# Four-layer graph network: early steps of layer 1 ahead of its norm, checks of layer 2 in other places, and a hyperbolic preparation with X0's numbers on GpSimd

## The chip, the cores and the metric

The kernel runs on one core of a Trainium2 chip. Five engines work side by side, each with a queue of its own that it takes in order: PE (TensorE, matrix products and transposes), ACT (ScalarE, activations with function tables that are loaded in sets), DVE (VectorE), POOL (GpSimd) and SP (SyncE, which issues most transfers). The metric is the device time of one execution in microseconds, the median of several runs. The profile describes one other execution.

## The reference, cut to what matters

Four layers share one adjacency matrix of 3327 by 3327 zeros and ones (0.5% ones) and a feature matrix x of 3327 by 64. Each layer normalizes x, clips it at zero, computes something over the graph and adds it to x.

```
h = relu(layernorm(x)); x = x + hyperbolic(h, adj, att_W, att_b)      # layer 0
h = relu(layernorm(x)); x = x + decay(h, adj, weight, bias)           # layer 1
h = relu(layernorm(x)); x = x + gat_and_gru(h, adj, adj, ...)         # layer 2
h = relu(layernorm(x)); x = x + hyperbolic(h, adj, r, w_att, b_att)   # layer 3

# hyperbolic: attention over pairs, times the hyperbolic logarithm of each pair
adj_att = sigmoid(left + right.T) * adj
support = einsum('ij,ijd->id', adj_att, logmap(x[:, None, :], x[None, :, :]))
return proj(expmap(x, support))

# decay: neighbours weighted by 0.5 to the power of how many neighbours come after them (at most 100)
w = mask * where(pos > 0, 0.5 ** (k - pos), 0);  return w @ (h @ weight) + bias

# gat_and_gru: sums over neighbours without the diagonal; two GRU cells
node_support = [(A > 0) @ h, (A < 0) @ h]
edge_output = gru_cell(node_support, h, ...)
node_output = gru_cell(softmax over neighbours @ (h @ W), h, ...)
return d_edge * edge_output + d_node * node_output
```

## The kernel before, in words

The 3327 nodes are padded to 3328 = 26 tiles of 128 (T = 26, P = 128, D = 64). The kernel takes a fast path that holds for an adjacency of zeros and ones and for small numbers; flags that this path collects (`zo`, `ok`) decide at the end whether its result stands, and a general path follows in the program otherwise.

**Layers 0 and 3** are `hyperbolic_series`. A preparation normalizes, makes two half-precision parts of the features (`hi`, `lo` in `Xp`), transposes them tile by tile on PE into `XT` (7 groups of four tiles, each copied out of PSUM by ACT or DVE in turn), computes the time-like coordinate X0 of every point and its half-precision parts on DVE (`of_x0`, `of_e`, `of_f`, L454 to L470), transposes these into `XE`, makes `left` and `right`, spreads `left` over all partitions with PE (`of_left`, L514 to L522), and computes seven small numbers per node that are needed at the end of the layer (L538 to L544). `keep_busy` issues products whose result nobody reads. After it runs a loop over 104 pieces (4 column chunks, 26 row tiles): sigmoid on ACT (L575), times the mask on POOL (L577), products on PE (L588, L589), a square on ACT (L595), two operations on DVE (L600, L601), sums on PE (L610, L618). A short tail of small operations ends the layer; in layer 3 it calls Tanh and then loads the table of Sqrt (L739 to L742).

**Layer 1** is `plain_decay`. It runs over 52 steps, 2 column halves by 26 row tiles from the last to the first. In each step DVE makes a mask from a loaded piece of the adjacency (L1326) and tests the same piece for zeros (`zeros`, L1248). PE counts neighbours with a triangular matrix (L1333, `after` and `rest`), ACT takes 2 to the power of minus the count (L1339, an Exp), PE sums (L1350). For 13 of the 52 steps (`LATE` = 0, 1, 7, 11, ... 47) the test for zeros is left out here. Ahead of the steps stands the norm (`norm_relu`, L131 to L143), which goes from DVE to ACT (Square, L135; Sqrt, L98) and back. The pieces are loaded seven ahead.

**Layer 2** is `plain_gat`. It has its own norm, then on PE 26 products with the masks (L1518, in order of falling b), in between small jobs from a table `todo`: transposes (`turn`), degrees (`degrees`) and their inverse (`inverse`, on ACT with Relu, Ln and Exp and the table of Sigmoid afterwards). The 13 tests that layer 1 left out are done here, one at every even b, from pieces loaded again into three buffers. Behind them come the GRU steps u = 0 to 7, which begin with `take` (L1538, L1539): it moves the sums out of PSUM, on ACT and on DVE.

The order of instructions on ACT, DVE, PE and (in the first two) POOL is that of the source inside a block `tc.manual_schedule`; outside of such blocks, and between them, a scheduler places what is ready. An ACT instruction that needs another function set gets a table load in front, which the building of the program puts there. `table_of` (L117 to L119) issues a one-element activation only to have a table loaded early:

```
def table_of(f, after=None):
    A.activation(spare, one_c if after is None else after, f)
```

Of the kernel before, what the change touches and what calls it, by code (L numbers as in the profile page):

```python
# [46 lines left out]
def tile_gnn4(ctx: ExitStack, tc: tile.TileContext, x, adjT, att0, b0, w1, bias1, w_gat, a_gat,  # L47
# [274 lines left out]
    def hyperbolic_series(r, params, ok, masks=None, done=None):  # L322
# [18 lines left out]
        with ExitStack() as st:  # L341
# [53 lines left out]
            with tc.tile_pool(name="hsp", bufs=1) as tp, tc.tile_pool(name="hsps", bufs=2, space=PSUM) as ps, \  # L395
                    tc.manual_schedule(engines={mybir.EngineType.Activation, mybir.EngineType.DVE,
                                                mybir.EngineType.PE, mybir.EngineType.Pool}):
                Xe = tp.tile([P, T, KE + 9], F16, name="Xe")
# [11 lines left out]
                H, R, sq, sr = [tp.tile([P, T, D], F32, name=n) for n in ("H", "R", "sq", "sr")]  # L410
# [43 lines left out]
                def of_x0():  # L454
                    V.scalar_tensor_tensor(x0, x2, 1.0, ia, op0=OP.add, op1=OP.mult)
                    V.tensor_scalar(x0s, x0, SX, None, op0=OP.mult)
                    V.tensor_copy(p0[:, :, 0], x0s)
                    V.tensor_sub(rest, x0s, p0[:, :, 0])
                    V.tensor_copy(p0[:, :, 1], rest)
                    V.tensor_sub(rest, rest, p0[:, :, 1])  # L460
                    V.tensor_copy(p0[:, :, 2], rest)

                def of_e():
                    for k, src in ((0, h0.to_broadcast([P, T, 3])), (3, m0.to_broadcast([P, T, 2])), (5, l0)):
                        V.tensor_copy(E[:, :, k:k + src.shape[-1]], src)

                def of_f():
                    for k, src in ((0, p0), (3, hm0), (5, h0)):
                        V.tensor_scalar(Fe[:, :, k:k + src.shape[-1]], src, -1.0, None, op0=OP.mult)
                    G.tensor_copy(F, Fe)  # L470
# [7 lines left out]
                def to_columns16(dst, src, rows, odd, between=()):  # L478
                    between = list(between)
                    for t0 in range(0, T, 4):  # L480
                        n = min(4, T - t0)
                        pt = ps.tile([P, 4 * P], F16, name="pt", bufs=4)
                        for k in range(n):
                            PE.transpose(pt[:rows, k * P:(k + 1) * P], src[:, t0 + k, :], ident_h)  # L484
                        if t0 // 4 % 2 == odd:
                            V.tensor_copy(dst[:, t0 * P:(t0 + n) * P], pt[:rows, :n * P])
                        else:
                            A.activation(dst[:, t0 * P:(t0 + n) * P], pt[:rows, :n * P], AF.Copy)
                        if between:
                            between.pop(0)()  # L490

                junk, pe = [ps.tile([P, W], F32, name=n, bufs=1) for n in ("junk", "pe")]

                def keep_busy(n):

                    for _ in range(n):
                        PE.matmul(junk, ident_h, hi[:, :8, :], start=True, stop=True)

                keep_busy(4)
                to_columns16(XT, Xp[:, :, :2 * D], P, 1,  # L500
                             (of_x0, of_e, of_f, lambda: V.tensor_copy(Xe[:, :, :D], hi), of_z))
                columns(chunks[0])

# [8 lines left out]
                c = chunks[0]  # L512

                def of_left():  # L514

                    for o, to in ((0, junk), (1, pe)):
                        for i in range(c[1]):
                            t = o * HT + c[0] + i
                            PE.matmul(to[:, i * P:(i + 1) * P], left[:, t:t + 1].to_broadcast([P, P]), ident,
                                      start=True, stop=True)  # L520
                    V.tensor_copy(leftB[c][:, 0, :], junk[:, :c[1] * P])
                    A.activation(leftB[c][:, 1, :], pe[:, :c[1] * P], AF.Copy)  # L522

                to_columns16(XE, Xe, KE + 9, 0, (lambda: None, of_left))
                for o in range(2):
                    pt = ps.tile([P, 4 * P], F16, name="pt", bufs=4)
                    for i in range(c[1]):
                        PE.transpose(pt[:KE, i * P:(i + 1) * P], Xp[:, o * HT + c[0] + i, D:], ident_h)
                    V.tensor_copy(XF[c][:, o, :], pt[:KE, :c[1] * P])
                PE.transpose(pe[:T, :P], left, ident)  # L530
                keep_busy(6)
                A.activation(LT, pe[:T, :P], AF.Copy)
                nc.sync.dma_start(left_row, LT)
                V.tensor_copy(X0[:, :, 0], x0)
                V.scalar_tensor_tensor(good, x2, X2_MIN, nodes, op0=OP.is_ge, op1=OP.mult)
                V.reduce_sum(ok, good, axis=AX.X)
# [7 lines left out]
                V.tensor_scalar(small["bh"], ax, 0.5, isqc, op0=OP.mult, op1=OP.mult)  # L544

# [143 lines left out]
            with tc.tile_pool(name="hse", bufs=1) as tp:  # L689
# [28 lines left out]
                if r is None:  # L718


                    f = MIN_NORM
                    by, g = new("by"), new("g")
                    V.tensor_scalar(by, v2, -f * f, 1.0, op0=OP.mult, op1=OP.add)
                    V.tensor_scalar(g, by, MIN_NORM, None, op0=OP.max)
                    V.reciprocal(g, g)
                    V.tensor_mul(t, root, g)
                    A.activation(th, t, AF.Tanh)
                    V.tensor_mul(th, th, rr)
                    V.tensor_mul(y2, th, th)
                    stt(vh, vh, 2.0 * f, th, op0=OP.mult, op1=OP.mult)  # L730
                    V.tensor_mul(y2, y2, x2)
                    stt(d, v2, f * f, y2, op0=OP.mult, op1=OP.mult)
                else:

                    V.tensor_scalar(t, v2, 1e-8, None, op0=OP.max)
                    ti = inverse_root(tp, t, "ti")
                    V.tensor_mul(t, t, ti)
                    V.tensor_scalar(t, t, um, None, op0=OP.max)
                    A.activation(th, t, AF.Tanh)  # L739
                    table_of(AF.Sqrt, th[:, :1])  # L740
                    V.reciprocal(ti, t)
                    V.tensor_mul(th, th, ti)  # L742
                    V.tensor_mul(y2, th, th)
                    stt(vh, vh, 2.0, th, op0=OP.mult, op1=OP.mult)
                    V.tensor_mul(y2, y2, v2)
                    V.tensor_mul(d, y2, x2)
# [526 lines left out]
    def plain_decay(masks, zo, deg, wt, bias, gru, ball_of_r):  # L1273
# [11 lines left out]
        with ExitStack() as st:  # L1285
# [24 lines left out]
            with tc.tile_pool(name="pdacc", bufs=1, space=PSUM) as pa, tc.manual_schedule(  # L1310
# [54 lines left out]

                K_ = len(steps)
                make_mask(0)
                make_mask(1)
# [15 lines left out]
                for o in range(2):  # L1384
                    cnt[o] = pa.tile([P, 2, 512], F32, name=f"cnt{o}")
                for k in range(K_ + 2):
                    c, b = steps[min(max(k, 0), K_ - 1)]
                    if 0 <= k < K_:
                        counts(k, 0, after)
                        weights(k, 0)  # L1390
                    if 0 <= k - 1 < K_:
                        counts(k - 1, 1, rest)
                        if steps[k - 1][1] == 0:
                            degrees(steps[k - 1][0], 1)
                    if 0 <= k < K_:
                        counts(k, 1, after)
                        weights(k, 1)
# [4 lines left out]
                    if 0 <= k < K_:  # L1402
# [7 lines left out]
                    if k == 1:  # L1410
                        late()
# [19 lines left out]
    def plain_gat(masks, zo, deg, first, wg, gru):  # L1431
# [8 lines left out]
        with ExitStack() as st:  # L1440
# [10 lines left out]
            wk = st.enter_context(tc.tile_pool(name="pgl", bufs=3))  # L1451
# [4 lines left out]
            with tc.tile_pool(name="pgp", bufs=1) as tp, tc.tile_pool(name="pgacc", bufs=1, space=PSUM) as pa, \  # L1456
# [4 lines left out]

                hn = tp.tile([P, T, D], F32, name="hn")
# [25 lines left out]
                def degrees(k):  # L1488

                    cs = slice(k * BK, (k + 1) * BK)  # L1490
# [4 lines left out]
                    V.tensor_sub(deg[:, cs], deg[:, cs], dg)  # L1495

                def inverse():
# [8 lines left out]
                    table_of(AF.Sigmoid, r0[:, :1])  # L1506
                    V.scalar_tensor_tensor(deg, deg, -1.0, r0, op0=OP.mult, op1=OP.mult)
                    V.scalar_tensor_tensor(deg, deg, 2.0, r0, op0=OP.add, op1=OP.mult)

                todo = {T - 4: lambda: turn(0), T - 6: lambda: degrees(0), T - 8: lambda: turn(4),  # L1510
                        T - 9: lambda: degrees(1), T - 11: lambda: turn(8), T - 12: lambda: degrees(2),
                        T - 14: lambda: turn(12), T - 15: lambda: degrees(3), T - 17: inverse}
                for b in range(T - 1, -1, -1):
# [9 lines left out]
                    if b % 2 == 0:  # L1523
                        same = wk.tile([P, 2, CW], BF, name="same", bufs=1)
                        k = LATE[(T - 1 - b) // 2]
                        zeros(same, late.pop(0), zo[:, k:k + 1])


# [173 lines left out]
```

## Time and profile before

| | |
|---|---|
| median of 3 runs | 819.15 us (821.02, 819.15, 817.87) |
| profiled execution, its own time | 818.34 us |
| span of its instructions | 816.6 us |
| mean granted TensorE clock | 0.924 of full speed |
| busy: PE, DVE, ACT, POOL | 81%, 87%, 71%, 51% |
| layer 0: preparation, loop, tail | 0 to 35, 35 to 264, 264 to 284 us |
| layer 1 | 284 to 425 us |
| layer 2 | 428 to 527 us |
| layer 3: preparation, loop, tail | 529 to 560, 560 to 789, 790 to 811 us |

All times inside the span are microseconds from its start. In a row of a timeline the first number is the start, the second the busy time (of all that are merged in the row), then engine, line, operation, output <- input, shapes and how often; in brackets the idle time of the engine before it and what released it. Rows of neighbouring like instructions are merged, so a row can reach past the start of the next.

### The profile page before, as it was taken

The numbers are of one execution on the slowest core, as the hardware profiler recorded it, in microseconds if no ns is written. First come the engines' busy times: TensorE is split into PE (matmuls) and PEld (weight loads), VectorE is DVE, ScalarE is ACT, GpSimd is POOL, SyncE is SP. The second block draws the span as 40 slices with busy tenths as digits, with TensorE's granted clock in tenths as the row PEclk, the third lists the DMA queues.
The fourth block names the chain that finished last, engine by engine and source line by source line (L and its number), as shares of the span: only waits on it lengthen the run. The fifth ranks groups of instructions, "written<-read, shape, count | busy, mean of one in ns | idle before, by whom it ended". The sixth has DMA issues, their size and how long they took to land. (4 is left out here: it accounts for less than half of the span.)

```text
span 816.6 us, 11802 instructions
## 1 busy us (share of the span) xinstructions
PE 659.8 (81%) x4215; PEld 252.1 (31%) x4215; DVE 709.1 (87%) x985; ACT 576.2 (71%) x729; POOL 416.1 (51%) x296
## 2 busy tenths in 40 slices
PE   0799999999999049989993995427999999999960
PEld 0522233333332024435441651214222333333320
DVE  6789999989998899998967567996899999999976
ACT  2678888878886367777782575255888888888862
POOL 2299988989987050003120000004687777787730
PEclk9989999999999569999996997757999999999995
DMA  3567676776664739998913541001001001000001
GB/s 75 164 203 219 205 212 184 205 213 196 196 189 120 292 131 327 372 379 298 367 36 132 187 151 50 1 4 45 1 1 34 1 1 36 1 1 2 1 2 46
DMA packets 57621, 107.84 MB, mean 132 GB/s; under 512 B 8752, under 2 KB 33488, under 8 KB 57552
## 3 DMA queue, kind: packets, MB, share of 16 engines
q1 hardware_dynamic: 53200, 106.97, 40.5%
q10 hardware_dynamic: 4352, 0.02, 0.3%
q8 instruction: 35, 0.57, 0.3%
q14 instruction: 34, 0.28, 0.1%
HBM read 103.72 MB, written 0.88 MB: 128 GB/s over the span
## 5 line engine op out<-in xcount | busy, mean ns | idle before, releaser
L595 ACT ACTIVATE y<-slot,shift_c 128x768 f32<-128x768 f32 (+1 forms) x208 | 197.4, 949 | 68.4 <-ACT sig L575 48.6
L601 DVE TENSOR_TENSOR sig<-slot,sig 128x768 f32<-128x768 f32 (+1 forms) x208 | 213.2, 1025 | 23.3 <-POOL sig L577 2.1
L600 DVE SCALAR_TENSOR_TENSOR slot<-y,slot 128x768 f32<-128x768 f32 (+1 forms) x208 | 212.1, 1020 | 9.1 <-ACT y L595 9.0
L577 POOL TENSOR_TENSOR sig<-adj,sig 128x768 f32<-128x768 f32 (+1 forms) x104 | 201.9, 1962 | 28.1 <-ACT sig L575 26.0
L575 ACT ACTIVATE sig<-leftB,right 128x768 f32<-128x768 f32 (+1 forms) x208 | 204.1, 981 | 3.5 <-DVE bh L544 3.5
L577 POOL TENSOR_TENSOR sig<-mask,sig 128x768 f32<-128x768 fp8e4 (+1 forms) x104 | 174.6, 1680 | 61.6 <-ACT sig L575 57.6
L610 PE MATMUL slot<-sig,Xr 128*64 128x384 f32 (+1 forms) x832 | 188.3, 541 | 16.8 <-DVE sig L601 16.8
L588 PE MATMUL slot<-XC,XT 128*128 128x384 f16 (+1 forms) x416 | 142.9, 344 | 5.2 <-DVE sig L601 3.5
L589 PE MATMUL slot<-XF,XE 73*128 73x384 f16 (+1 forms) x416 | 142.0, 341 | 0.0
L1339 ACT ACTIVATE w<-cnt,ebias 128x832 bf16<-128x832 f32 x104 | 93.7, 950 | 30.7 <-PE cnt L1333 30.7
L1248 DVE TENSOR_SCALAR_CACHE_REDUCE same<-adj 128x1664 bf16<-128x1664 f32 x52 | 97.5, 1876 | 3.6 <-DMA adj<-in 3.4
L618 PE MATMUL slot<-sig,X 128*32 128x384 f32 (+1 forms) x832 | 96.0, 533 | 0.0
L610 PEld LDWEIGHTS slot<-sig,Xr 128*64 128x64 f32 x832 | 43.1, 135 | 122.5 <-DVE sig L601 83.4
L1333 PE MATMUL cnt<-mask,after 128*128 128x416 fp8e4 x208 | 54.8, 347 | 22.7 <-DVE mask L1326 19.8
L588 PEld LDWEIGHTS <-XT 128*128 128x128 f16 x416 | 40.8, 98 | 96.1 <-issue 70.7
L191 POOL TENSOR_TENSOR mask<-mask,offdiag 128x128 fp8e4<-128x128 fp8e4 x26 | 15.0, 594 | 97.9 <-PE cnt L1333 97.9
L1333 PE MATMUL cnt<-mask,rest 128*128 128x416 fp8e4 x208 | 54.7, 345 | 10.2 <-ACT w L1339 10.2
L400 POOL MEMSET X<- 128x832 f32 x2 | 1.6, 794 | 115.0 <-PE pt L1234 115.0
L1326 DVE TENSOR_SCALAR mask<-adj 128x1664 fp8e4<-128x1664 f32 x52 | 52.9, 1035 | 0.0
L589 PEld LDWEIGHTS <-XE 73*128 73x128 f16 x416 | 40.9, 98 | 33.6 <-issue 9.9
L1350 PE MATMUL acc<-w,h 128*64 128x416 bf16 x416 | 46.6, 345 | 0.0
L1518 PE MATMUL bank<-mask,h 128*64 128x416 fp8e4 x416 | 39.7, 348 | 0.0
(299 smaller groups left out, 521.8 us busy)
## 6 DMA issues: line engine op xcount, KB each, us to landing
adj<-in SPq DMA_DIRECT2D x65, 832.0 KB, 6.6
adj<-in SPq DMA_DIRECT2D x78, 384.0 KB, 3.9
adj<-in SPq DMA_DIRECT2D x27, 512.0 KB, 4.4
leftB<-left SPq DMA_DIRECT2D x6, 384.0 KB, 3.5
XC<-XT SPq DMA_DIRECT2D x12, 96.0 KB, 4.3
X<-in SPq DMA_DIRECT2D x2, 416.0 KB
out<-X SPq DMA_DIRECT2D x2, 416.0 KB, 2.4
XF<-XT SPq DMA_DIRECT2D x6, 96.0 KB, 2.6
```

Of the source, the lines that this page charges most:

```text
L575: A.activation(sig, leftB[c], AF.Sigmoid, bias=right[:, b:b + 1])
L577: G.tensor_tensor(sig, adj, sig, op=OP.mult)
L588: PE.matmul(L[:, o, :c[1] * P], XT[:, rows], XC[c][:, o, :], start=True, stop=False)
L589: PE.matmul(L[:, o, :c[1] * P], XE[:KE, rows], XF[c][:, o, :], start=False, stop=True)
L595: A.activation(ys[k], Ls[k][:, :, :c[1] * P], AF.Square, scale=-0.5 / SX ** 2, bias=shift_c)
L600: V.scalar_tensor_tensor(L, y, G3, L, op0=OP.add, op1=OP.mult)
L601: V.tensor_mul(sig, L, sig)
L610: PE.matmul(acc[c][o * D:(o + 1) * D, 0, :n], Xr[:, b, :], sigs[k][:, o, :], start=b == 0, stop=b == T - 1)
L618: PE.matmul(acc[c][q:q + 32, 1, :n], X0[:, b - 1 + i, :], w[:, o, :], start=b == 1, stop=b == T - 1, tile_position=(0, q))
L1248: V.tensor_scalar(same, adj, 0.0, 0.0, op0=OP.is_equal, op1=OP.add, accum_out=count)
L1333: PE.matmul(cnt[o][:, h, :BK], w, cols(k, o, h), start=w is after and steps[k][1] == T - 1, stop=True, skip_group_check=True)
L1339: A.activation(ws[k][:, o, :, :], cnt[o][:, :, :BK], AF.Exp, scale=-LN2, bias=ebias)
```

## The change

In the preparation of layers 0 and 3, X0's numbers (before: 13 DVE operations and one POOL copy between XT's evictions) become 15 POOL operations that start ahead of the transposes. The groups of XT come in one piece, evicted by ACT and DVE in turn. The groups of XE are evicted by ACT (0 to 2) and, behind the spread of `left`, by DVE (3 to 6). The seven end numbers stand ahead of that spread. Products that nobody reads go from 4 and 6 to 2 and 0. The transposed `left` is copied by DVE instead of ACT.

In `plain_decay`, counts and weights of steps 0 and 1 stand ahead of the norm, with a table load of Exp before them and one of Sqrt after; `late` comes one step later, the rest of the loop is the same. In `plain_gat` the buffers for reloaded pieces are four instead of three, the 13 tests stand at four places (4, 3, 4, 2), degrees go in pairs, and the inverse comes at b = 15 instead of 9. In the tail of layer 3 the product after Tanh has a tile of its own.

```diff
                 def of_x0():
-                    V.scalar_tensor_tensor(x0, x2, 1.0, ia, op0=OP.add, op1=OP.mult)
-                    V.tensor_scalar(x0s, x0, SX, None, op0=OP.mult)
-                    V.tensor_copy(p0[:, :, 0], x0s)
...
+                    G.tensor_scalar(x0, x2, 1.0, None, op0=OP.add)
+                    G.tensor_tensor(x0, x0, ia, op=OP.mult)
+                    G.tensor_scalar(x0s, x0, SX, None, op0=OP.mult)
+                    G.tensor_copy(p0[:, :, 0], x0s)
+                    G.tensor_tensor(rest, x0s, p0[:, :, 0], op=OP.subtract)
+                    G.tensor_copy(p0[:, :, 1], rest)
+                    G.tensor_tensor(rest, rest, p0[:, :, 1], op=OP.subtract)
+                    G.tensor_copy(p0[:, :, 2], rest)
+                    for k, src in ((0, p0), (3, hm0), (5, h0)):
+                        G.tensor_scalar(Fe[:, :, k:k + src.shape[-1]], src, -1.0, None, op0=OP.mult)
+                    G.tensor_copy(F, Fe)
                     for k, src in ((0, h0.to_broadcast([P, T, 3])), (3, m0.to_broadcast([P, T, 2])), (5, l0)):
-                        V.tensor_copy(E[:, :, k:k + src.shape[-1]], src)
+                        G.tensor_copy(E[:, :, k:k + src.shape[-1]], src)
...
-                keep_busy(4)
-                to_columns16(XT, Xp[:, :, :2 * D], P, 1,
-                             (of_x0, of_e, of_f, lambda: V.tensor_copy(Xe[:, :, :D], hi), of_z))
+                of_x0()
+                for _ in range(2):
+                    PE.matmul(junk, ident_h, hi[:, :8, :], start=True, stop=True)
+                groups = range(0, T, 4)
+                for t0 in groups:
+                    to_columns16(XT, Xp[:, :, :2 * D], P, t0, (A, V)[t0 // 4 % 2])
                 columns(chunks[0])
+                of_z()
+                V.tensor_copy(Xe[:, :, :D], hi)
...
+                for t0 in groups[:3]:
+                    to_columns16(XE, Xe, KE + 9, t0, A)
                 V.tensor_mul(root, root, zs)
...
+                for t0 in groups[3:]:
+                    to_columns16(XE, Xe, KE + 9, t0, V)
+                PE.transpose(junk[:T, :P], left, ident)
+                V.tensor_copy(LT, junk[:T, :P])
...
                     table_of(AF.Sqrt, th[:, :1])
                     V.reciprocal(ti, t)
-                    V.tensor_mul(th, th, ti)
+                    ta, th = th, new("th_t")
+                    V.tensor_mul(th, ta, ti)
...
-                make_mask(0)
-                make_mask(1)
+                for o in range(2):
+                    cnt[o] = pa.tile([P, 2, 512], F32, name=f"cnt{o}")
+                table_of(AF.Exp)
+
+                def counts_before(k):
+                    counts(k, 0, after)
+                    weights(k, 0)
+                    if k:
+                        counts(k - 1, 1, rest)
+                        if steps[k - 1][1] == 0:
+                            degrees(steps[k - 1][0], 1)
+                    counts(k, 1, after)
+                    weights(k, 1)
+
+                for k in range(2):
+                    make_mask(k)
+                    counts_before(k)
+                    counts(k, 0, rest)
+                table_of(AF.Sqrt)
                 H = pers.tile([P, T, D], F32, name="H")
...
                     norm_relu(tp, H, order=(1, 0), then=after_norm)
-                for o in range(2):
-                    cnt[o] = pa.tile([P, 2, 512], F32, name=f"cnt{o}")
-                for k in range(K_ + 2):
+                sums(0)
+                for k in range(2):
+                    make_mask(k + 2)
+                    load(k + AHEAD)
+                for k in range(2, K_ + 2):
...
-            wk = st.enter_context(tc.tile_pool(name="pgl", bufs=3))
+            wk = st.enter_context(tc.tile_pool(name="pgl", bufs=4))
...
+                def check(n=1):
+                    for _ in range(n):
+                        same = wk.tile([P, 2, CW], BF, name="same", bufs=1)
+                        k = LATE[len(LATE) - len(late)]
+                        zeros(same, late.pop(0), zo[:, k:k + 1])
...
                     A.activation(r0, r0, AF.Exp, scale=-1.0)
                     table_of(AF.Sigmoid, r0[:, :1])
+                    check(4)
                     V.scalar_tensor_tensor(deg, deg, -1.0, r0, op0=OP.mult, op1=OP.mult)
                     V.scalar_tensor_tensor(deg, deg, 2.0, r0, op0=OP.add, op1=OP.mult)
-                todo = {T - 4: lambda: turn(0), T - 6: lambda: degrees(0), T - 8: lambda: turn(4),
-                        T - 9: lambda: degrees(1), T - 11: lambda: turn(8), T - 12: lambda: degrees(2),
-                        T - 14: lambda: turn(12), T - 15: lambda: degrees(3), T - 17: inverse}
+                    check(len(late))
+                todo = {T - 2: lambda: check(4), T - 4: lambda: turn(0), T - 6: lambda: degrees(0, 1),
+                        T - 7: lambda: check(3), T - 8: lambda: turn(4), T - 10: lambda: degrees(2, 3),
+                        T - 11: inverse, T - 12: lambda: turn(8), T - 15: lambda: turn(12)}
...
-                    if b % 2 == 0:
-                        same = wk.tile([P, 2, CW], BF, name="same", bufs=1)
-                        k = LATE[(T - 1 - b) // 2]
-                        zeros(same, late.pop(0), zo[:, k:k + 1])
```

## The prediction

> **What bounds the kernel now.** I read the page's busy shares first, then the chain of waits that ended last, then the timeline of one engine at a time through the places that the diff touches.
>
> ```profile
> span 816.6 us, 11802 instructions
> PE 659.8 (81%) x4215; PEld 252.1 (31%) x4215; DVE 709.1 (87%) x985; ACT 576.2 (71%) x729; POOL 416.1 (51%) x296
> DVE 31%; PE 7%; ACT 4%; issue 3%; DMA 1%; DVEq 0%; SPq 0%; ACTq 0%
> ```
>
> VectorE (DVE) is busy most, but the average covers six stretches: layer 0's preparation to 35, its loop to 264, its end to 284, layer 1 (`plain_decay`) to 425, layer 2 (`plain_gat`) to 527, layer 3 again like layer 0. The two hyperbolic loops (229 us each) are not edited. What counts is where DVE stands still or stands in the way, between them.
>
> The first such place is the start of the GRU in layer 2: DVE's timeline, start and length.
>
> ```profile
> 484.53 1.88 DVE L1248 TENSOR_SCALAR_CACHE_REDUCE same<-adj 128x1664 bf16<-128x1664 f32 x1
> ...
> 495.61 1.89 DVE L1248 TENSOR_SCALAR_CACHE_REDUCE same<-adj 128x1664 bf16<-128x1664 f32 x1 [2.35 <-DMA adj<-in]
> 497.43 1.58 DVE L1539 SCALAR_TENSOR_TENSOR deg<-bank,deg 128x416 f32<-128x416 f32 x3
> ```
>
> PE's neighbour sums end at 484.5, but `take` (L1539) waits in DVE's queue behind five checks of adj (L1248), two of which wait for their load. ScalarE shows the same hole:
>
> ```profile
> 486.73 1.28 ACT L1565 ACT_TABLE_LOAD   x1
> ...
> 498.05 1.11 ACT L1544 ACTIVATE xh<-deg 64x416 f32<-64x416 f32 x2 [6.95 <-DVE deg L1539]
> ```
>
> The second is the head of layer 1 (ScalarE, then PE):
>
> ```profile
> 288.97 1.83 ACT L135 ACTIVATE ln_sq<-H 128x832 f32<-128x832 f32 x2 [9.13 <-DVE H L134]
> 292.11 0.23 ACT L98 ACTIVATE ln_sd<-ln_v 128x26 f32<-128x26 f32 x1 [1.30 <-DVE ln_v L138]
> ...
> 295.80 1.78 ACT L1339 ACTIVATE w<-cnt,ebias 128x832 bf16<-128x832 f32 x2
> ```
> ```profile
> 314.18 0.51 PE L1333 MATMUL cnt<-mask,after 128*128 128x416 fp8e4 x2 [0.24 <-DVE mask L1326]
> ```
>
> The norm is a chain DVE, ScalarE, DVE; then masks pace PE until 314.18, after which PE and ScalarE go at 2.335 us a step with nothing to spare. The third is the end of each preparation, where the first sigmoid waits for DVE's last small number, and the fourth a product in the tail behind a table load:
>
> ```profile
> 35.15 1.15 ACT L575 ACTIVATE sig<-leftB,right 128x1024 f32<-128x1024 f32 x1 [1.73 <-DVE bh L544]
> ...
> 798.50 0.19 DVE L742 TENSOR_TENSOR th<-th,ti 128x26 f32<-128x26 f32 x1 [1.46 <-ACT spare L119]
> ```
>
> **The change, part by part.**
>
> **Layer 2 (−9.1).** The thirteen checks (1.88 each, 24.5 in sum) are not removed, they are spread: four after b=24, three after b=19, four between ScalarE's Exp and the two products that use it, two at the end. With the sums at 1.57 us per b from 443.7, DVE's order gives: 4 checks 443.7–451.3; two subtractions of the degrees, waiting for their b, to 455.8; 3 checks to 461.5; two subtractions 462.7; maximum 463.9; ScalarE's Relu, Ln, Exp with their tables (7.6 us in the trace, 473.19 to 480.77) to 471.6, DVE's 4 checks under it 464–471.6; products to 475.4; 2 checks to 479.4. That is 5 us before the sums end. The loads they need run on SP's queue; one more buffer (3 to 4) lets them go earlier, and the last four are asked for when the third check frees its buffer. `take` then follows the sums' eviction on ScalarE (484.58–491.1, unchanged, with the table load in its middle): DVE's takes 485.8–491.7, products(1) on PE done by 492.8, the second GRU step's first DVE operation at 493.05. Before it stood at 502.28, so −9.2; one step later, by the gates (503.39 before, 495.0 after), −8.4, from where DVE is contiguous at 2.95 us a step. I take −9.1. The cover is the 5 us; if it is gone, each later us costs one.
>
> **Head of layer 1 (+3.0).** Counts and the four Exp of steps 0 and 1 move ahead of the norm on PE and ScalarE. They need masks 0 and 1, which DVE has at 285.8 as before. Queued behind them on ScalarE is the norm's Square. In the trace these four Exp with their PE steps take 295.80 to 300.71, 4.9 us; from 285.95 they end at 290.85. Then table_of(Sqrt): load 1.28 and spare 0.20, 292.35. Square starts there instead of 288.97: +3.4. DVE has nothing else in its queue, so the variance sum moves 289.90 to 293.27, and everything behind (root, relu, split, masks 2 on) with it. Back comes about 0.4: the twelve bias adds of POOL run from 293.22 under DVE's work, which they slow (relu 1.25 us there); part of them falls into the idle. What the two steps save PE and ScalarE comes too early: PE waits for masks up to 314.18, that time moves by 3, and the rate afterwards is 2.335 with DVE at 2.29, so nothing is recovered. +3.0, between 2.0 (DVE's 0.045 a step over the layer's 46 remaining steps pays half) and 3.7.
>
> A rule speaks louder against this part. The row: a load takes 1.28 and the next ACTIVATE starts 0.01 later (486.73 to 488.02). The Trainium skill, "ScalarE: Activation LUTs", section "What ACT_TABLE_LOAD costs", says a switch costs the load plus about 1.38 us of drain, 2.66. By it the head would be +4.4 and the next item +2.7; no load in this trace shows the drain, so I take the row, and keep 2.8 more as the range's far end.
>
> **Layer 0's preparation (+1.05).** The built order of the changed kernel shows what the diff does not: `plain_decay`'s table_of(Exp) needs nothing, and as first ScalarE instruction of its ordered block it is placed in layer 0's preparation, between ScalarE's second and third eviction of XT. The same happens in the trace to layer 3's Sqrt (482.30, with the sigmoid table loaded again at 486.73). So the first sigmoid's table must be loaded again, after its waits: +1.28 in the open. Around it: of_x0, of_e, of_f (13 DVE operations, 22.16–24.6) become 15 on POOL from 17.6. POOL's rows (F copy 0.41, small ones 0.19 to 0.27) sum to about 5.2, ready at 23, needed at 26.65: hidden, with 3.6 to spare. XT's evictions then end at 26.25 (24.9 without the extra load), pw's reduce comes at 26.7 for 27.65, left at 27.25, 12 transposes of XE to 28.4, the broadcast of left to 31.4, and after it leftB, two XF, four XE, LT, X0, good, ok end at 34.4; the seven end numbers (33.88–35.03 before) lie under the broadcast. The sigmoid could go 0.65 earlier; with the reload it comes at 35.8, +0.65.
>
> The other rule against the change: "SBUF — State Buffer", section "Who interferes with whom", has a DVE instruction with two SBUF inputs and a POOL one that reads SBUF lock each other out. Beside the new POOL chain stand four wide ones (Xr, lo). By the rule each may wait for a whole POOL operation, about 0.3, or POOL for all four (4 us, which eats the 3.6 spare). The row nearest is relu, 1.25 beside POOL's adds against 1.03 without: +0.2. I take 0.4 per layer, ends 0 and 1.2.
>
> **Layer 3's preparation (−0.5).** The same without a misplaced load: the sigmoid at 559.5 for 560.37, −0.9, plus 0.4. Fewer spare products (10 to 2) could leave PE's clock lower at each loop's start; with them the slices at the loops' starts already show 8 tenths in layer 0, 5 and 7 in layer 3. I take 0, ends 0 and +1.9 a loop (DVE waited 1.88 there in layer 3).
>
> **Tail (−1.45).** DVE's product no longer writes the tile that ScalarE's Sqrt reads: 798.50 becomes 797.05 (Tanh ends 796.97). All behind it is one chain.
>
> Sum: +1.05 +3.0 −9.1 −0.5 −1.45 = −7.0. The profiled execution's span goes from 816.6 to 809.6, its own time from 818.34 to 811.3; it stands 0.8 below the median of the runs, 819.15, which becomes 812.1.
>
> **Rivals.** (A) The two early steps pay: PE's lead of two steps (4.7) outlasts the masks' delay, because DVE skips `same` at several early steps. Then layer 1 gives 0 to −4.7 in place of +3: 804.4 to 809.1. For: DVE is idle at the head anyway. Against: PE waits for masks at 314.18. (B) Slower: the checks still end after the sums. Loads in layer 2 are the place: the last one took 7.13 us to land before (488.37 to 495.5), and DVE's checks now stand in front of the degrees' subtractions, which feed the inverse. At 479.4 they have 5 us of cover; past 484.5 they delay, and the gain of 9.2 with −1.95 elsewhere pays the +4.05 until they end at about 491.5; from there the change loses, past 496 by 4: 820 to 824. Against: thirteen loads of 832 KB need 30 us at layer 1's 2.3 each, and have 36. (C) The GRU's start is bound by ScalarE's queue: evictions, table load, gates and tanh stand there in one row, busy from 484.58 to 491.1 before the DVE wait begins. Then DVE is ready and waits, and half of layer 2's gain is lost, +4.5: 816.6, hardly a change. For: ScalarE then has the takes of the second GRU too (1.1 each). Against: once running, DVE's 2.95 a step is the longer one.
>
> **How the numbers follow.** About 0.5% (815.05 to 823.25) is what a measurement of this kernel tells from no change. As worked, with 809 to 815: 0.63. A: 0.15. C: 0.17. B: 0.05. Faster 0.78, same 0.17, slower 0.05. The predicted time is that of the likeliest, 812.1. For 8 in 10 I reach into half of A, 806.5, and to C's value, 816.5; the likeliest alone has 809 to 815.
>
> **What would show it.** The table load before the first sigmoid, and an Exp load among the XT evictions; Square of layer 1 at about 293; no `same` after 484; the second GRU step's first operation about 9 us after the sums' end instead of 18; L742's product 0.1 after Tanh. It is wrong if layer 1 is not longer, if checks wait for loads before the inverse, or if the loops' first tiles are slower.

## The result, and the profile after

The changed kernel takes 810.52 us (median of 4 runs, 809.51 to 811.12), the kernel before 820.03 in the same comparison (817.87 to 821.02): ratio 0.9891, 95% interval 0.987 to 0.9911: 1.1% less, clear of the noise. Forecast were 812.1, with 806.5 to 816.5 as range. The span of the profiled execution goes from 816.6 to 808.8, by 7.8; forecast were 7.0. That the total agrees says less than it seems, as the single stretches show.

Between events that both traces have, the spans differ as follows (start of the event after, less the same before; "forecast" are the terms of the prediction's sum):

| stretch, from event to event | before | after | difference | forecast |
|---|---|---|---|---|
| layer 0 to mask 0 of layer 1 | 283.85 | 281.59 | −2.26 | +1.05 |
| layer 1: mask 0 to ScalarE's table load at its end | 143.23 | 149.10 | +5.87 | +3.0 |
| to the first sum of layer 2's norm | 2.56 | 4.03 | +1.47 | 0 |
| norm and neighbour sums, to the first xh copy | 54.94 | 54.73 | −0.21 | 0 |
| GRU, to the first sum of layer 3 | 46.55 | 37.45 | −9.10 | −9.1 |
| layer 3's preparation, to its first sigmoid | 29.24 | 27.19 | −2.05 | −0.5 |
| layer 3's loop, to the first copy of its sums (L628, after L622) | 229.15 | 229.26 | +0.11 | 0 |
| tail, to ScalarE's root L109 of n | 12.41 | 11.05 | −1.36 | −1.45 |
| rest | 14.67 | 14.40 | −0.27 | 0 |
| sum | 816.6 | 808.8 | −7.8 | −7.0 |

Two terms are as worked out (GRU, tail), two are off by about 3 in opposite directions (layers 0 and 1), and layer 3's preparation is off by 1.5.

The GRU's start after, on DVE's timeline (start, length, engine, line, operation):

```profile
481.72 1.89 DVE L1243 TENSOR_SCALAR_CACHE_REDUCE same<-adj 128x1664 bf16<-128x1664 f32 x1
...
483.64 0.21 DVE L1666 TENSOR_REDUCE ok<-zo 128x1 f32<-128x54 f32 x1
490.53 0.59 DVE L1562 SCALAR_TENSOR_TENSOR deg<-bank,deg 128x416 f32<-128x416 f32 x1 [6.68 <-ACT xh L1561]
...
496.51 0.64 DVE L1594 SCALAR_TENSOR_TENSOR nn<-bank,gb,gate 128x416 f32<-128x416 f32 x1
...
497.75 0.65 DVE L1594 SCALAR_TENSOR_TENSOR nn<-bank,gb,gate 128x416 f32<-128x416 f32 x1
```

The last check ended at 483.61 and a small reduction at 483.85; then DVE is idle for 6.68 in front of `take` (here L1562), and `take` waits for ScalarE's copy, as forecast. No check waits for its load any more: the idle time in front of all 52 checks of the kernel goes from 3.6, of which 3.4 was waiting for loads, to 0.3. The second GRU step's first operation comes 8.3 after the first xh copy (489.45); before it came 17.7 after it.

ScalarE's timeline through layer 0's preparation:

```profile
23.58 1.28 ACT L119 ACT_TABLE_LOAD   x1
24.88 0.20 ACT L119 ACTIVATE spare<-one_c 128x1 f32<-128x1 f32 x1
...
29.20 0.60 ACT L525 ACTIVATE leftB<-pe 128x512 f32<-128x512 f32 x1 [0.72 <-PE pe L522]
32.05 1.28 ACT L569 ACT_TABLE_LOAD   x1 [2.25 <-DVE ok L538]
33.34 1.15 ACT L569 ACTIVATE sig<-leftB,right 128x1024 f32<-128x1024 f32 x1
```

Layer 1's Exp load stands at 23.58 between the evictions of XT, and the sigmoid's table is loaded again at 32.05, after the wait for DVE's `ok`: both as forecast. But `ok` itself, ending at 31.95, is much earlier than the forecast 34.4; 1.5 of this is PE's clock (see `again`).

And the head of layer 1 on ScalarE, then the tail on ScalarE and DVE:

```profile
287.66 0.95 ACT L1334 ACTIVATE w<-cnt,ebias 128x832 bf16<-128x832 f32 x1 [0.40 <-PE cnt L1328]
288.62 1.28 ACT L119 ACT_TABLE_LOAD   x1
289.91 0.20 ACT L119 ACTIVATE spare<-one_c 128x1 f32<-128x1 f32 x1
290.02 1.67 ACT L135 ACTIVATE ln_sq<-H 128x832 f32<-128x832 f32 x2
```
```profile
790.56 0.23 ACT L733 ACTIVATE th<-t 128x26 f32<-128x26 f32 x1 [0.24 <-DVE t L732]
...
790.98 0.19 DVE L737 TENSOR_TENSOR th_t<-th,ti 128x26 f32<-128x26 f32 x1
```

Square comes at 290.02, 8.43 after mask 0; before, 5.12 after it. That is +3.31 (forecast +3.4). In the tail the product L737 starts 0.19 after the end of Tanh (790.79) instead of 1.54 after it, and no longer waits for a table load. ScalarE's root L109 comes at 794.40 instead of 801.93; 1.36 of that arises inside the tail.

### The profile page after: what moved, and what is told of

Read it like the earlier page. It is cut to its first block, busy times and chain, and to the rows that moved or that the text cites. A ratio compares the mean times of both kernels' runs of the same rounds, so it can differ in the third digit from the quotient of the medians.

```text
span 808.8 us, 11770 instructions
## 1 busy us (share of the span) xinstructions
PE 659.7 (82%) x4199; PEld 252.1 (31%) x4199; DVE 705.3 (87%) x961; ACT 581.0 (72%) x733; POOL 425.9 (53%) x324
## 5 line engine op out<-in xcount | busy, mean ns | idle before, releaser
L1328 PE MATMUL cnt<-mask,after 128*128 128x416 fp8e4 x208 | 56.6, 356 | 22.8 <-DVE mask L1321 19.9
L1345 PE MATMUL acc<-w,h 128*64 128x416 bf16 x416 | 49.3, 360 | 9.9 <-ACT h L183 9.4
```

What stands on the lines that cost most here:

```text
L1328: PE.matmul(cnt[o][:, h, :BK], w, cols(k, o, h), start=w is after and steps[k][1] == T - 1, stop=True, skip_group_check=True)
```

## The experiments

The changed kernel was run once more, and eleven variants of it. The medians are of several executions, each group with runs of the kernel before beside it, and the ratios are against these. All other times are from the profile of one execution each.

| run | median, before's | ratio, interval | first sigmoid | layer 1 | GRU | prep. 3 |
|---|---|---|---|---|---|---|
| before | | | 35.15 | 143.23 | 46.55 | 29.24 |
| changed | 810.52, 820.03 | 0.9891, 0.9870 to 0.9911 | 33.34 | 149.10 | 37.45 | 27.19 |
| again | 809.64, 818.69 | 0.9896, 0.9872 to 0.9919 | 34.81 | 147.63 | 37.46 | 27.14 |
| no_exp | 808.65, 818.69 | 0.9872, 0.9847 to 0.9896 | 33.49 | 148.89 | 37.46 | 27.09 |
| no_head | 806.19, 818.69 | 0.9846, 0.9806 to 0.9886 | 33.59 | 144.86 | 37.45 | 27.00 |
| head_sq | 808.00, 818.69 | 0.9872, 0.9847 to 0.9897 | 33.78 | 145.33 | 38.55 | 26.89 |
| no_gat | 818.19, 819.43 | 0.9981, 0.9966 to 0.9995 | 33.44 | 149.16 | 46.12 | 25.58 |
| no_prep | 815.11, 819.43 | 0.9940, 0.9919 to 0.9960 | 36.92 | 149.20 | 37.47 | 30.10 |
| warm | 804.98, 819.43 | 0.9821, 0.9799 to 0.9843 | 33.76 | 143.26 | 38.58 | 26.88 |
| x0_dve | 809.47, 819.43 | 0.9876, 0.9851 to 0.9901 | 35.79 | 144.56 | 37.48 | 29.97 |
| best | 802.18, 819.27 | 0.9798, 0.9771 to 0.9826 | 32.14 | 143.25 | 36.28 | 26.99 |
| head_one | 803.36, 819.27 | 0.9807, 0.9779 to 0.9836 | 33.73 | 143.30 | 36.27 | 28.19 |
| skips_best | 802.24, 820.39 | 0.9783, 0.9752 to 0.9815 | 33.55 | 142.39 | 36.30 | 27.06 |
| skips_head | 800.14, 820.39 | 0.9765, 0.9731 to 0.9799 | 33.52 | 141.81 | 36.29 | 27.07 |

"Prep. 3" is layer 3's preparation to its first sigmoid. Layer 1 is followed best by the start of ScalarE's first weight in each step, counted from mask 0, less the same before. The column halves change between steps 25 and 26 (the "half change" below).

| run | step 7 | step 26 | step 29 |
|---|---|---|---|
| changed | 3.02 | 3.02 | 5.88 |
| again | 3.02 | 3.03 | 4.40 |
| no_exp | 3.01 | 3.02 | 5.66 |
| no_head | 0.00 | 0.00 | 1.63 |
| head_sq | 2.06 | 2.11 | 2.11 |
| no_gat | 3.02 | 3.02 | 5.92 |
| no_prep | 3.02 | 3.07 | 5.97 |
| x0_dve | 0.00 | 0.00 | 1.32 |
| warm | 0.02 | 0.03 | 0.03 |
| best | 0.01 | 0.01 | 0.01 |
| head_one | 0.01 | 0.07 | 0.07 |
| skips_best | −1.38 | −1.38 | −1.38 |
| skips_head | −2.00 | −1.95 | −1.96 |

So layer 1's +5.87 has two parts: 3.02, which is there at step 7 and doesn't change until step 26, and 2.86 at the half change.

### again

Nothing is edited.

> The changed kernel once more, unaltered, for a second profile. In its first profile PE's granted clock is halved from 362.6 to 369 us, at the change of the column halves in layer 1, and layer 1 loses 2.9 us there; the kernel before shows full clock at that place with the same idle gaps (1.04 and 1.84). Theory 'place': the loss hangs on where the program stands when the gaps come, and so it returns at the same place, span 808.8 within 0.5. Rival 'chance': the clock's windows lie differently in each execution, the loss is absent or elsewhere, and the span moves by 2 to 3.

The head's 3.02 returns to the hundredth. The loss at the half change returns smaller, 1.37 for 2.86; the 1.47 in front of layer 2's norm is gone (2.56 as before), and layer 0's first sigmoid is 1.47 later. Each of these goes with PE's granted clock. Windows of the changed kernel's first execution, then of the kernel before, each with its length, the busy time (and number of instructions) of PE, its weight loads, DVE, ScalarE and POOL, then the granted clock, DMA share and GB/s:

```profile
362.00:366.00 4.00, 2.76 (x12) 0.90 (x12) 4.00 (x4) 2.85 (x6) 0.00 (x0) 0.57 1.02 406
366.00:370.00 4.00, 4.00 (x18) 1.53 (x17) 3.85 (x6) 2.08 (x3) 0.41 (x1) 0.58 1.01 389
```
```profile
362.00:366.00 4.00, 3.52 (x26) 1.53 (x25) 4.00 (x6) 3.39 (x7) 0.41 (x1) 1.00 1.02 399
366.00:370.00 4.00, 4.00 (x28) 1.84 (x28) 3.15 (x4) 2.92 (x4) 0.68 (x2) 1.00 1.03 382
```

With the clock at half, PE does 30 products in these 8 us instead of 54 (a part of the second gap lies in them too). In front of it PE had stood for 1.04 and 1.84, waiting for ScalarE's copies of the degrees. Both gaps are in both kernels; these rows are of the changed one:

```profile
360.53 0.51 PE L1328 MATMUL cnt<-mask,after 128*128 128x416 fp8e4 x2 [1.04 <-ACT deg L1350]
...
363.24 0.85 PE L1328 MATMUL cnt<-mask,after 128*128 128x416 fp8e4 x2 [1.84 <-ACT deg L1350]
```

The rival "chance" of this run is nearer to what was seen than "place": the gaps are always there, the loss is 0 to 2.9. In front of layer 2's norm it is the same: in every profile PE stands for 1.78 at the end of layer 1, for ScalarE's last copy, and in four of the fourteen (changed, no_gat, no_prep, skips_best) the clock is halved behind it and the norm comes 1.3 to 1.5 later. The same in layer 0's preparation: in the changed kernel's first profile the clock was full while `left` was spread (2.00 from the first to the last of its products), in the second it was mostly at half (3.37), as in the profile before (2.91). So 1.5 of the −2.26 of layer 0 is such luck, and so are 2.86 + 1.47 of what was lost from layer 1 on.

### no_exp

```diff
-                table_of(AF.Exp)
 
                 def counts_before(k):
```

> The changed kernel without the one-element Exp at the head of layer 1, whose table load stands in layer 0's preparation. Theory: the first sigmoid's reload (1.28) goes, the first sigmoid comes 1.28 earlier and everything after it, span 807.5; layer 1's own Exp load stays hidden at its old place before the first weights. If in addition the clock's loss at the half change depends on the moment, it may go too: 804.7. Rival: the reload is hidden (DVE's first operation of the loop waits for POOL or PE anyway): span unchanged, 808.8.

The reload is gone and the first sigmoid comes at 33.49, where `again`, with the same halved clock in the preparation, had 34.81: 1.32 for the 1.28 expected. From the end of `ok` to the sigmoid it is 0.11 instead of 1.40. The load's own place, among the evictions of XT, cost nothing: the reduction of pw starts at 26.27 without it and at 26.25 with it. And it bought nothing: in both kernels the Exp table is loaded once more for the first weights (277.81 here), hidden in a wait of 4.82. The whole span is only 0.5 shorter than again's: its half change cost 2.65 and again's 1.37, and other stretches differ by up to 1.1 either way.

### no_head

```diff
-                for k in range(2):
-                    make_mask(k)
-                    counts_before(k)
-                    counts(k, 0, rest)
-                table_of(AF.Sqrt)
+                make_mask(0)
+                make_mask(1)
...
```

> The changed kernel with layer 1 as before (masks 0 and 1, norm, then all steps); all else stays. Theory: the head costs 3.0 by Square's lateness and 1.28 by the Exp load: span 804.5; and 801.7 if the 2.9 of lost clock at the half change belong to the head. Rival (A of the prediction, early steps pay): the span grows above 808.8.

The rest of the edit puts the loop of layer 1 back as it was before. The 3.02 is gone entirely and 1.63 of clock loss stays; span 802.5. By the medians too it is faster than `again` (806.19 and 809.64, measured together). The rival, early steps that pay, falls: without them layer 1 is shorter.

### head_sq

```diff
-                table_of(AF.Exp)
...
                     counts(k, 0, rest)
-                table_of(AF.Sqrt)
```

> The changed kernel without both one-element activations around the early steps (Exp and Sqrt): the early weights stay ahead of the norm, Square follows them at once, and the Sqrt table is loaded between Square and the root, under the variance sum. Theory: Square 1.4 earlier, first sigmoid 1.28 earlier, span 806.1 with the clock's loss and 803.2 without. Rival: the load in front of the root is in the open, and Square's gain is lost: 807.5.

Square comes 7.10 after mask 0 instead of 8.43, so 1.33 earlier where 1.4 was expected, and the Sqrt load lies under the variance sum. By step 7 the gain is down to 0.96 (2.06 instead of 3.02); where the rest went was not followed up. In this execution the half change cost nothing although the two gaps were there, and the GRU lost 1.1 to a halved clock instead (warm's GRU, 38.58, shows the same).

### warm

```diff
+                    if k == T:
+                        nxt = [pa.tile([P, BK], F32, name=f"acc{h}", bufs=2) for h in range(2)]
+                        spare_products(nxt, 4)
                     if 0 <= k < K_:
                         counts(k, 0, after)
...
+                    if k == T:
+                        spare_products(nxt, 8)
                     if 0 <= k < K_:
                         counts(k, 1, after)
```

> Layer 1 as before in the changed kernel (as in no_head), with twelve products on PE whose result nobody reads, four and eight, in PE's two gaps of 1.04 and 1.84 at the change of the column halves. Theory: the gaps are what halves PE's clock there in some executions (1.5 to 2.9 us lost in layer 1); filled, the clock stays at 1.00 there and layer 1 takes 143.2 to 143.6 as in the profile before, where no_head took 144.9. Rival: the halving has nothing to do with the gaps and comes again; or the products delay the counts by 1 and more.

The diff is against no_head, on which this run is built. Layer 1 takes 143.26. The gaps shrink to 0.34 and 0.44 and the clock stays whole (windows as above):

```profile
362.00:366.00 4.00, 4.00 (x28) 1.84 (x28) 4.00 (x4) 3.46 (x6) 0.69 (x2) 1.00 1.03 404
366.00:370.00 4.00, 4.00 (x31) 2.19 (x32) 1.48 (x3) 2.99 (x4) 0.56 (x2) 1.00 0.95 336
```

Five kernels were run with these twelve products (warm, best, head_one, skips_best, skips_head), and none of their profiles has a loss at the half change; of the nine profiles without them seven have it, 1.3 to 2.9 each. That the gaps are needed for the loss is shown by this; what decides in which executions it comes is not (the kernel before and head_sq had the gaps and no loss). The Trainium skill, "TensorE: Matmul & The Clock Gate", Part 1, describes it so: the clock follows activity in windows of 3.4 us that run freely and do not start with the kernel. The halved stretches here fit with one or two such windows (by the granted clock in slices of 2 us, 3.4 us from 34.9 in layer 0 and 6.8 us from 362.6 in layer 1, both in the changed kernel's first profile). But the gaps, 1.04 and 1.84, are shorter than a window even together, so less than a whole idle window is enough here.

### no_gat

```diff
-            wk = st.enter_context(tc.tile_pool(name="pgl", bufs=4))
+            wk = st.enter_context(tc.tile_pool(name="pgl", bufs=3))
...
-                todo = {T - 2: lambda: check(4), T - 4: lambda: turn(0), T - 6: lambda: degrees(0, 1),
+                todo = {T - 4: lambda: turn(0), T - 6: lambda: degrees(0), T - 8: lambda: turn(4),
...
+                    if b % 2 == 0:
+                        same = wk.tile([P, 2, CW], BF, name="same", bufs=1)
...
```

> The changed kernel with layer 2 as before (three buffers, one check at every even b, degrees one by one, inverse at b = 9). Theory: the whole 9.1 between the end of the neighbour sums and the start of layer 3 comes from the checks that stand in front of take: that stretch goes from 37.45 back to 46.5, span 817.5 or so, no gain left but prep's and tail's against the head's cost. Rival: the fourth buffer or the clock makes part of it; then the stretch is shorter than 45.

The stretch is 46.12 again, so layer 2's part of the change is worth 8.7 to 9.1, and without it nearly nothing is left: ratio 0.9981. The run takes back all of that part at once (the places of the checks, the fourth buffer, the pairs of degrees, the place of the inverse); whether the places alone would do with three buffers was not tried. (Its preparation of layer 3, 25.58, had the clock at full during the spread of `left`: another 1.5.)

### no_prep

```diff
-                of_x0()
-
-                for _ in range(2):
-                    PE.matmul(junk, ident_h, hi[:, :8, :], start=True, stop=True)
+                keep_busy(4)
+                to_columns16(XT, Xp[:, :, :2 * D], P, 1,
+                             (of_x0, of_e, of_f, lambda: V.tensor_copy(Xe[:, :, :D], hi), of_z))
...
```

> The changed kernel with the hyperbolic preparation as before in both layers, and all else as changed. Theory: layer 3's preparation goes from 27.1 back to 29.2 (+2.1), and layer 0's first sigmoid from 34.8 to 36.4 (before's 35.15 and the Exp reload 1.28): span +3.7, about 811.5. Rival of the prediction's sum (preparation worth 0.65 and 0.9 less 0.4 each): +0.75 in both together.

The first sigmoid comes at 36.92, 2.1 later than in `again`; layer 3's preparation takes 30.10, 3.0 longer. Of these 0.2 and 0.7 are PE's clock: the products that spread `left` took 3.58 and 3.72 here, 3.37 and 2.98 in `again`. By the ratios (0.9940 beside 0.9891 and 0.9896) the two preparations are worth 3.6 to 4.0 together. That is the theory's 3.7, and several times the 0.75 of the prediction's sum.

### x0_dve

```diff
-                    G.tensor_tensor(x0, x0, ia, op=OP.mult)
-                    G.tensor_scalar(x0s, x0, SX, None, op0=OP.mult)
+                    V.tensor_tensor(x0, x0, ia, op=OP.mult)
+                    V.tensor_scalar(x0s, x0, SX, None, op0=OP.mult)
...
                 columns(chunks[0])
+                of_x0()
                 of_z()
...
```

> As no_head, with X0's numbers on DVE instead of POOL, behind the evictions of XT; the rest of the new order stays. Theory (POOL carries the gain): 14 small operations of DVE, 2.3 in sum, stand in front of z, Xe and the reduction of pw, so the preparation is 2.3 longer in each layer, span 807.1. Rival (the order of evictions and end numbers carries the gain, POOL's part was hidden): span as no_head, 802.5.

The preparations are 2.2 and 3.0 longer than in no_head, span 807.4: POOL carries the gain. It shows ahead of the spread of `left`, whose length hangs on the clock (2.0 at full in no_gat's layer 3, 3.7 at half in no_prep's): counted from the preparation's first sum, the reduction of pw is 2.5 later in both layers (24.38 for 21.89, 22.14 for 19.62). The new order, with X0's numbers on DVE in one piece behind the evictions, brings back what before had (first sigmoid 35.79, preparation 29.97, for 35.15 and 29.24).

### best

```diff
-                table_of(AF.Sqrt)
+                if masks is None:
+                    table_of(AF.Sqrt)
```

> As warm, without the one-element Sqrt at the head of layer 3's preparation: it is placed in layer 2 between the checks and take, its table is loaded in vain (the root of layer 3 loads it again), and the sigmoid's table is loaded again at the first gate of the GRU. Theory: the gate's reload (1.28) goes, the stretch from the end of the sums to layer 3 goes from 37.45 to 36.2 at full clock, layer 3's root is unchanged; median 803.7 beside warm's 805.0. Rival: DVE or the xh copies bound the GRU's start, and the stretch stays at 37.4.

The diff is against warm. The GRU stretch takes 36.28 (36.2 expected), with no table load left between the copies and the gates:

```profile
482.70 2.13 ACT L1559 ACTIVATE xh<-bank 64x416 f32<-64x416 f32 x4 [7.47 <-PE bank L1541]
484.85 1.21 ACT L1586 ACTIVATE gate<-bank,gs 128x416 f32<-128x416 f32 x2
```

This also bears on the prediction's rival C: once the checks are out of the way, ScalarE's copies and this load do set the GRU's start, but the change's 9.1 was reached with them. The median is 802.18 beside 804.98 of warm (with 819.27 and 819.43 for the kernel before).

### head_one

```diff
+                make_mask(0)
+                for o in range(2):
+                    counts(0, o, after)
+                    weights(0, o)
+                counts(0, 0, rest)
+                make_mask(1)
...
```

> As best, with step 0 alone ahead of layer 1's norm: its two weights end before Square is ready, and the Sqrt table is loaded under the variance sum. Theory (masks pace the first steps, PE and ScalarE the rest): Square is not late, layer 1's relu comes 9.9 after mask 0 as before, and PE's lead of one step (2.3) shrinks to what DVE lets through, 1 to 2 us: layer 1 takes 141.3 to 142.3. Rival: masks alone set the pace from step 2 on to the end; layer 1 stays at 143.3.

The diff is against best, and the loop of layer 1 starts one step later to match. Square is not late, the Sqrt load lies under the variance sum, the norm is as before:

```profile
287.24 1.83 ACT L135 ACTIVATE ln_sq<-H 128x832 f32<-128x832 f32 x2 [1.20 <-DVE H L134]
289.09 1.28 ACT L98 ACT_TABLE_LOAD   x1
290.39 0.23 ACT L98 ACTIVATE ln_sd<-ln_v 128x26 f32<-128x26 f32 x1
```

And yet layer 1 takes 143.30. The theory falls and the rival holds: the lead that the early step gives is 1.15 at step 2 and 0 at step 4. PE waits for the masks of steps 4 to 7 in this kernel as well, the last time here:

```profile
312.47 0.51 PE L1329 MATMUL cnt<-mask,after 128*128 128x416 fp8e4 x2 [0.24 <-DVE mask L1322]
```

That is 30.35 after mask 0; before it was 30.33 (314.18). A lead that ends in a wait for the same mask is worth nothing.

### skips_best and skips_head

```diff
-    LATE = 0, 1, *range(7, 2 * T - 4, 4)
+    LATE = 0, 1, 3, 5, *range(9, 2 * T - 10, 4)
```

The first has this edit on best, the second on head_one.

> As best, with another choice of the 13 steps whose check is put off: 0, 1, 3, 5, 9, 13 and so on to 41, instead of 0, 1, 7, 11 and so on to 47. Theory: PE's waits for the masks of steps 4 to 7 (0.24 each and what they hide, 0.4 a step) shrink, layer 1 is 1 shorter than 143.3: 142.3, and DVE still ends ahead of PE. Rival: the last ten steps without a skip make DVE late at the end, layer 1 is longer.

> As head_one, with that same choice of steps. Theory (a lead of PE is worth what the masks of the first steps let through): with two more skips before step 7 the lead of one step survives in part, layer 1 takes 141.0 to 142.0, at least 0.5 less than skips_best. Rival: an early step is worth nothing with these masks either; both take the same.

With two of the early checks put off, PE has no wait for a mask at steps 4 to 7, layer 1 is 0.9 shorter (142.39), and now the lead of one step pays another 0.6 (141.81). Both end 0.5 worse than they stood at step 40 (−1.38 becomes −0.84, −1.96 becomes −1.41): the last ten steps have no skip, and PE waits for a mask again there, 136.84 and 136.27 after mask 0. skips_head has the lowest time here: 800.14, ratio 0.9765 (0.9731 to 0.9799), against 0.9891 (0.987 to 0.9911) for the change as it was. Its interval overlaps with those of best, head_one and skips_best, so the order among these four rests on the stretches of single profiles.

## Why the prediction was right, and where it was not

**Layer 2, −9.1: right, by its own steps.** The checks ended 5.8 before the first xh copy (5 forecast), `take` waited for ScalarE, and the stretch became 9.10 shorter. no_gat gives it back. The rival B (checks still running after the sums, or waiting for loads) is not seen; of the rival C, ScalarE's queue, best shows the table load's 1.2, and the 9.1 was reached with it.

**Head of layer 1, +3.0: right.** 3.02 in every execution with the full head, 0.00 without it. The reason is the one forecast: Square stands behind four Exp and a table load (8.43 after mask 0 for 5.12), and PE's lead is lost to the masks by step 7, after which nothing recovers (3.02 at step 7 and at step 26). head_one confirms the second half by a case where Square isn't late. The 0.4 that was to come back is there too, by a longer way. In the changed kernel two small operations of DVE are slower beside POOL's bias adds, and the relu comes not 3.3 but 3.63 later:

```profile
293.96 0.35 DVE L101 TENSOR_TENSOR ln_sd<-ln_sd,ln_sd_r 128x26 f32<-128x26 f32 x1
294.35 0.37 DVE L102 TENSOR_SCALAR ln_sd<-ln_sd 128x26 f32<-128x26 f32 x1
```

Before they took 0.19 and 0.18. But the adds are then over earlier in the chain: the second relu and the masks 2 and 3 take 1.02 each instead of 1.27, 1.27 and 1.13, and 0.6 comes back.

**The Exp load in layer 0, +1.28: right.** 1.32 in no_exp against again, 1.29 counted from the end of `ok`.

**The preparations, −0.65 and −0.9, with +0.4 each for contention: wrong in size.** This is the step that failed; its direction was right. Two terms were mis-sized: the place of the twelve transposes of XE in the chain, and the contention. Without the Exp load and with a halved clock as before, the first sigmoid comes at 33.5 to 33.6, so −1.6, where −0.25 was said; in layer 3 −2.05, where −0.5 was said. The chain in no_head, on PE:

```profile
26.39 1.01 PE L480 MATMUL pt<-ident_h,Xe 128*82 128x128 f16 x12 [1.58 <-DVE Xe L497]
27.19 2.02 PE L522 MATMUL junk<-ident,left 128*128 128x128 f32 x8
29.00 1.69 PE L522 MATMUL pe<-ident,left 128*128 128x128 f32 x8
```

The reduction of pw came at 26.16 instead of 26.7. The forecast had the transposes behind `left`, until 28.4; they ran beside the reduction and `left`, so the spread of `left` began at 27.19, 1.2 earlier. It ended at 30.69 instead of 31.4, and `ok` at 33.47 instead of 34.4. The contention on DVE, 0.4 a layer, is next to nil: its four wide operations take 3.97 beside POOL's, 3.93 before. What the rule weighed there speaks of is seen in the trace, but with POOL as the one that loses (POOL's timeline after; DVE's four wide operations run from 18.17 to 22.16):

```profile
20.31 0.97 POOL L459 TENSOR_TENSOR rest<-x0s,p 128x26 f32<-128x26 f32 x1
21.34 0.91 POOL L460 CAST p<-rest 128x26 f16<-128x26 f32 x1
22.33 0.24 POOL L461 TENSOR_TENSOR rest<-rest,p 128x26 f32<-128x26 f32 x1
22.64 0.23 POOL L462 CAST p<-rest 128x26 f16<-128x26 f32 x1
```

The same kinds of operation take 0.97 and 0.91 beside DVE's wide ones and 0.24 and 0.23 alone. POOL's chain ends at 25.07, not 23: of the 3.6 to spare 2.1 are used, and nothing waits for it. The prediction had this as its far end ("POOL for all four") and took the middle, which neither engine paid.

**Tail, −1.45: right** (−1.36).

**What the sum didn't have: PE's clock inside layers 0, 1 and 2.** It was thought of at the loops' starts only, as a loss from fewer spare products, and no such loss is seen (layer 3's loop 229.26 for 229.15). It took 2.86 at the half change and 1.47 ahead of layer 2's norm and gave 1.47 in layer 0's preparation, in the one execution that was profiled. Which execution was profiled is luck here. So the close agreement of the totals (−7.0 and −7.8) comes partly from errors that cancel: preparations that are worth about 2.9 more than was said, against 2.9 net of lost clock. The other 0.8 lies in the loops (0.4 in layer 0's, 229.18 for 229.60, not traced to a cause) and the short stretches.

**The second rule weighed, a drain after each table load:** no. Wherever nothing else is waited for, the ACTIVATE behind a load starts 0.01 later in the traces before and after (288.62 + 1.28, then 289.91), and the reload at 32.05 cost 1.29 in all.

## What to carry to other kernels

Before work is moved ahead of a chain, look for what stands behind it in the same queue: two steps worth 4.7 of PE and ScalarE bought nothing, since the masks paced the start, and cost 3.0, since one small Square waited behind them. A one-element activation that only loads a table needs something to tie it to its place; without an input of its own it wanders ahead into another stage and costs a reload there (1.3 in layer 0, 1.2 at the GRU), which only the built order shows, not the diff. When a sum of terms agrees with a measurement, compare it stretch by stretch, and take a second profile of the same kernel before a difference of 1 to 3 us around PE's gaps is given a cause.

## What had not been expected of the hardware

Two gaps of PE of 1.04 and 1.84, ending 2.7 apart, were enough to halve its clock for 3 to 7 us in seven of nine executions, and twelve products without a use in these gaps avoided it in five of five. In the preparation it was POOL that lost beside DVE's wide operations with two inputs, about 0.7 an operation, and DVE next to nothing. In layer 1 both lost: beside each other DVE's relu took 1.28 for 1.02 and POOL's add 1.24 for 0.46, and two small operations of DVE took 0.35 and 0.37 for 0.19 and 0.18.
